# Three products and five adding transfers for each row, in place of four and four

## The chip, the cores and the metric

The kernel runs on one NeuronCore of one Trainium2 chip. The metric is the device time of one execution in microseconds (us), as the median of repeated runs. The engines are named as the profile names them: PE (TensorE, matrix products), PEld (its weight loads), DVE (VectorE), ACT (ScalarE), POOL (GpSimd) and SP (SyncE, here the issuer of plain DMAs).

## The reference, cut to what matters

The model takes 16 rows of 512 tokens with 128 channels through six residual steps. The change touches two of them, both calls of the same mixture of experts, one (k = 0) before a recurrence and one (k = 1) after it:

```python
def _L1_ffn_ref(x, gate_w, w1, w2):              # x: 16 rows x 512 tokens x 128
    scores = jnp.einsum('ntd,ed->nte', x, gate_w)
    probs = jax.nn.softmax(scores, axis=-1)
    g, m = jax.lax.top_k(probs.transpose(0, 2, 1), k)     # 128 of 512 tokens for each of 8 experts
    xin = x[batch_idx, m]
    h = jax.nn.gelu(jnp.einsum('nekd,edf->nekf', xin, w1), approximate=False)
    h = jnp.einsum('nekf,efd->nekd', h, w2)
    out_tok = g[..., None] * h
    return jnp.zeros((n, t, d), dtype=x.dtype).at[batch_idx, m].add(out_tok)
...
x = x + 0.5 * _L1_ffn_ref(_layernorm(x, axis=-1), ...)
```

So for each row and each of its eight experts: 128 chosen tokens are fetched, go through two products with a GELU between, are scaled by their gain, and are added back at the places that they came from.

## The kernel before, in words

The first part of the kernel (to about 970 us) does the attention and the small feed-forward networks of all rows. The change does not touch it. What follows is the expert stage: 2 layers x 16 rows x 8 experts = 256 jobs, and beside them, as side tasks, the recurrence of each pair of rows between the two layers and the routing of the second layer.

A job is one (k, b, e): layer, row, expert. It goes through four stations, one job behind the other, in a loop whose every round has three steps (the three `yield`s at L942, L957 and L988). First, POOL gathers the job's 128 tokens from HBM with an indirect DMA (L859, into xg; issued by `fetch`, ahead of time, about one for each round). PE transposes them two jobs at a time (L883, ps_x), ACT or DVE copies them to xin (L885). PE then makes ps_h (L935), ACT takes the GELU (L937), PE makes ps_y (L950), and ACT scales it by the gain (L953).

The result returns in one of two ways, which `by_product` decides:

- **By product**, for the experts e < EP of each row, and for all eight experts of the very last row. DVE builds a 0/1 matrix from the token numbers (L947), the result is split into three bf16 parts (ACT L953 and L941, DVE L959 and L956), and PE multiplies both in 12 small matmuls that add into the PSUM tile acc (L968). When the row's last product is in, DVE adds acc to x[b] (L972) and SP copies x[b] to a tile in HBM, sums[k, b] (L978).
- **By an adding transfer**, for the other experts. ACT leaves the result in ye, and POOL issues an indirect DMA that adds its 128 rows to sums[k, b] in HBM (L982). After the row's last one, `back` lets 18 steps pass and has SP bring the row back to SBUF (L918, k = 0, after which the row's recurrence may start) or copy it to the output (L923, k = 1).

The order of the jobs is a list that the program makes beforehand (L839 to L846): the products in their order, and behind each product a transfer, beginning EP + 1 products late, so that a row's transfers come after its products. With EP = 4 that is one product and one transfer in turn. Everything is issued in the order of this list: each engine's queue is in order, and the program's own schedule decides the order within it. POOL's queue holds the gathers, the scatters (the adding transfers), and of each normalisation the two steps L293 and L294, which wait for DVE's statistics (L291) and for which DVE's L304 waits. A normalisation of each row precedes its recurrence and another its second routing, four for each pair of rows.

ye has two sets of E - EP slots, used by even and odd rows (L952 and L984). Dependences, between DMAs that touch the same tile in HBM too, become semaphore waits on the queue of the engine that issues.

Of the kernel before, what the change touches and what calls it, by code (L numbers as in the profile page):

```python
# [31 lines left out]
E = 8  # L32
# [3 lines left out]
GB = 8  # L36
IN, OUT = 38, 8
LATE = 28
EP = 4
AHEAD = 4  # L40
EPS = 1e-5
NEG = -1.0e30
# [4 lines left out]
def tile_macaron(  # L47
# [51 lines left out]
    with ExitStack() as ph:  # L99
# [734 lines left out]
        def by_product(k, b, e):  # L834
            return e < EP or (k, b) == (1, B - 1)

# [4 lines left out]
        transfers = [job for job in every if not by_product(*job)]  # L841
        order = []
        for i, job in enumerate(products):
            order.append(job)
            if 0 <= i - EP - 1 < len(transfers):
                order.append(transfers[i - EP - 1])  # L846

        begun, fetched, moved = [0], [0], [0]

# [41 lines left out]
        def experts():  # L891
# [34 lines left out]
            while begun[0] < len(order) or any(line):  # L926
# [16 lines left out]
                if line[1]:  # L943
# [5 lines left out]
                    for f in range(NF):  # L949
                        nc.tensor.matmul(py, lhsT=hs[u][:, f, :], rhs=mw2[e][:, f, :],  # L950
                                         start=(f == 0), stop=(f == NF - 1))
                    yu = yes[u][:, 0, :] if prod[1] else ye[:, b % 2 * (E - EP) + e - EP, 0:D]  # L952
                    nc.scalar.activation(yu, py, AF.Copy, scale=gainT[g][:, n : n + 1])  # L953
# [7 lines left out]
                if prod[3]:  # L961
                    k, b, e, u = line[3]
                    last = E - 1 if (k, b) == (1, B - 1) else EP - 1
                    if e == 0:
# [14 lines left out]
                if line[2] and not prod[2]:  # L979
# [3 lines left out]
                        out=sums[k, b], out_offset=bass.IndirectOffsetOnAxis(ap=tokI[g][:, n : n + 1], axis=0),  # L983
                        in_=ye[:, b % 2 * (E - EP) + e - EP, 0:D], in_offset=None, compute_op=ALU.add,  # L984
                    )
# [244 lines left out]
```

## Time and profile before

| what | value |
|---|---|
| median of 3 runs | 1685.1 us (1683.93 to 1688.63) |
| the profiled execution's own time | 1679.07 us |
| its span, first to last instruction | 1677.3 us |
| granted TensorE clock, mean of the span | 0.979 |
| busy over the span: PE, DVE, ACT, POOL | 94%, 67%, 60%, 61% |
| L968, accumulating matmuls | 1584 (132 jobs x 12), 219 ns each |
| L982, scatters on POOL | 124, 1624 ns each |
| L859, gathers on POOL | 256, 986 ns each |
| first and last start of a scatter | 988.87 and 1667.34 us |

A group's mean duration is that of one instruction. Matmuls overlap in the pipeline, so their mean is longer than the distance between their starts. In a timeline, the brackets hold the time for which the engine stood idle before the instruction and what, by the semaphores, released it; "issue" means that nothing in the profile explains it. Where the named releaser had long been done, it was another, often a DMA.

The page's first two rows of tenths (40 slices of 41.9 us) show PE at nine tenths or more for nearly the whole span, and POOL rising in the expert stage:

```profile
PE   5689999999999999999999799999999999999998
...
POOL 2635557556665556565634757657766668667774
```

### The profile page before, as it was taken

To read this page: it belongs to the slowest core of one execution; us is meant where nothing else is said; L and a number is where in the kernel's file an instruction comes from. 1 tells how busy PE (TensorE), PEld (TensorE's weight loads), DVE (VectorE), ACT (ScalarE), POOL (GpSimd) and SP (SyncE) were. 2 spreads that over 40 slices of the span, in tenths; PEclk is the share of its full clock that TensorE was granted. 3 is DMA by queue.
4 is the path that set the end of the run, shared out by engine and by line. 5 is a ranking of instruction groups with operands and counts; after the bars stand their busy time and mean duration, and the time that the engine had idled before them with its cause. 6 is when DMAs were issued, how large, how long until landed. Compare 5 with 4: busy or idle time off the path is not lost.

```text
span 1677.3 us, 35404 instructions
## 1 busy us (share of the span) xinstructions
PE 1573.0 (94%) x12943; PEld 1093.7 (65%) x12943; DVE 1124.6 (67%) x3606; ACT 1002.3 (60%) x2000; POOL 1023.6 (61%) x1486
## 2 busy tenths in 40 slices
PE   5689999999999999999999799999999999999998
PEld 2234444444444544455444399888998889999998
DVE  6578878888888888888986146843469544672222
ACT  3446677787777877777777565444443434444454
POOL 2635557556665556565634757657766668667774
PEclk9779999999999999999999799999999999999999
DMA  4210111111101110111122114223323233333333
GB/s 123 67 63 26 56 50 40 33 42 57 53 30 40 49 57 23 40 52 56 35 81 62 30 40 78 58 52 76 64 59 64 58 61 73 67 64 75 70 77 58
DMA packets 103093, 94.87 MB, mean 57 GB/s; under 512 B 13197, under 2 KB 91478, under 8 KB 102678
## 3 DMA queue, kind: packets, MB, share of 16 engines
q1 hardware_dynamic: 76060, 67.65, 13.1%
q0 software_dynamic: 26048, 24.93, 9.4%
q8 instruction: 102, 1.67, 0.4%
q14 instruction: 73, 0.60, 0.1%
q10 hardware_dynamic: 810, 0.02, 0.0%
HBM read 59.00 MB, written 37.49 MB: 58 GB/s over the span
## 4 chain that ended last, share of the span: by engine, by line
PE 71%; DVE 19%; ACT 5%; issue 3%; POOL 2%; DMA 1%; DVEq 0%; SPq 0%; POOLq 0%; ACTq 0%
PE ps_h L935 12%; PE ps_y L950 11%; PE ps_av L692 7%; PE ps_st L669 6%; PE ps_sc L611 5%; DVE below L616 5%; PE acc L968 4%; PE ps_kg L365 4%; PE ps_s L338 3%; PE ps_t L318 3%; DVE ln_st L287 2%; ACT pt L672 2%; PE ps_ko L386 2%; PE ps_h L1076 2%; PE ps_h L1075 1%
## 5 line engine op out<-in xcount | busy, mean ns | idle before, releaser
L674 POOL TENSOR_SCALAR_AFFINE_SELECT pt<-pt 128x128 f32<-128x128 f32 (+2 forms) x704 | 252.7, 366 | 331.4 <-ACT pt L672 326.6
L672 ACT ACTIVATE pt<-ps_st 128x512 f32<-128x512 f32 (+1 forms) x704 | 378.8, 563 | 99.8 <-PE ps_st L669 94.0
L616 DVE CUSTOM_DVE_ANT_0 below<-ps_sc,causal 128x512 bf16<-128x512 f32 (+1 forms) x512 | 315.0, 615 | 80.1 <-PE ps_sc L611 64.8
L937 ACT ACTIVATE mo<-ps_h 128x512 f32<-128x512 f32 x256 | 152.8, 597 | 290.4 <-PE ps_h L935 288.5
L859 POOL DMA_INDIRECT xg<-xnd,tokI x256 | 252.3, 986 | 80.9 <-issue 45.0
L669 PE MATMUL ps_st<-qp,kp 99*128 99x512 bf16 (+3 forms) x1024 | 258.5, 305 | 21.7 <-ACT pt L672 20.8
L935 PE MATMUL ps_h<-xin,mw 128*128 128x128 f32 x2048 | 278.3, 279 | 0.0
L950 PE MATMUL ps_y<-mw,mo 128*128 128x128 f32 x2048 | 271.1, 275 | 0.4 <-DVE mo L959 0.4
L611 PE MATMUL ps_sc<-kp,qp 72*128 72x512 bf16 (+3 forms) x1024 | 259.6, 305 | 11.6 <-DVE maxs L616 6.6
L935 PEld LDWEIGHTS ps_h<-xin,mw 128*128 128x128 f32 x2048 | 249.7, 192 | 6.1 <-issue 3.2
L950 PEld LDWEIGHTS ps_y<-mw,mo 128*128 128x128 f32 x2048 | 249.1, 192 | 1.5 <-DVE mo L959 1.3
L982 POOL DMA_INDIRECT sum<-ye,tokI x124 | 201.4, 1624 | 63.4 <-ACT ye L953 22.7
L669 PEld LDWEIGHTS <-kp 99*128 99x128 bf16 x1024 | 95.1, 100 | 181.7 <-issue 164.4
L371 ACT ACTIVATE kan_h<-kan_s,rbias,kw 128x512 f32<-128x512 f32 x256 | 205.7, 812 | 3.8 <-PE ps_kg L365 3.8
L692 PE MATMUL ps_av<-pt,va 128*32 128x512 f32 (+3 forms) x2048 | 165.5, 441 | 0.0
L621 DVE TENSOR_REDUCE maxs<-ps_sc 128x2 f32<-128x512 f32 (+1 forms) x192 | 130.1, 685 | 34.9 <-PE ps_sc L611 34.4
L611 PEld LDWEIGHTS <-qp 72*128 72x128 bf16 x1024 | 96.2, 99 | 79.8 <-issue 57.2
L956 DVE TENSOR_TENSOR mo<-mo 128x128 bf16<-128x128 f32 x132 | 38.2, 290 | 129.4 <-ACT mo L941 129.1
L692 PEld LDWEIGHTS ps_av<-pt,va 128*32 128x32 f32 x2048 | 53.7, 109 | 94.9 <-issue 44.1
L968 PE MATMUL acc<-mo 128*128 128x128 bf16 x1584 | 111.3, 219 | 3.1 <-DVE mo L956 3.0
L968 PEld LDWEIGHTS <-mo 128*128 128x128 bf16 x1584 | 98.6, 98 | 19.9 <-issue 18.6
L294 POOL TENSOR_TENSOR ln_rstd<-ln_rstd,mhalf 128x4 f32<-128x4 f32 x96 | 101.1, 1053 | 8.0
(197 smaller groups left out, 2362.2 us busy)
## 6 DMA issues: line engine op xcount, KB each, us to landing
qp<-qs SPq DMA_DIRECT2D x64, 288.0 KB
xnd<-kan_x SPq DMA_DIRECT2D x32, 256.0 KB
sum<-x SPq DMA_DIRECT2D x31, 256.0 KB
qs<-qpart SPq DMA_DIRECT2D x48, 128.0 KB
kp<-ks SPq DMA_DIRECT2D x48, 96.0 KB
x<-in_L_attn_x_dram SPq DMA_DIRECT2D x16, 256.0 KB
mw<-in_L_ffn_w_dram SPq DMA_DIRECT2D x16, 256.0 KB
xg<-xnd,tokI POOLq DMA_INDIRECT x256
```

The lines of the kernel that those rows point to most:

```text
L371: nc.scalar.activation(h, sk[half], AF.Relu, bias=rbias[:, half, v : v + 1], scale=kw1[:, half, v : v + 1])
L611: nc.tensor.matmul(v[:, u, 0:n], lhsT=qp[r][0 : 9 * HD, g, bass.ts(c, P)], rhs=kp[0 : 9 * HD, r, 0:n], start=alone, stop=(u == len(gs) - 1 ...
L616: nc.vector.tensor_tensor_reduce(below[:, 0:n], v[:, 0, 0:n], causal[:, S - n : S], 1.0, LOWEST, ALU.add, ALU.max, accum_out=maxs[:, c, h ...
L669: nc.tensor.matmul(v[:, u, 0:n], lhsT=kp[ROWS, r, bass.ts(c, P)], rhs=qp[r][ROWS, g, c * P : S], start=True, stop=True)
L672: nc.scalar.activation(o, v[:, :, 0:n], AF.Exp, scale=HD ** -0.5)
L674: nc.gpsimd.affine_select(out=dg, in_=dg, compare_op=ALU.is_ge, fill=0.0, base=0, pattern=[[0, len(gs)], [1, P]], channel_multiplier=-1)
L692: nc.tensor.matmul(po[32 * g : 32 * g + 32, c * P : S], lhsT=va[:, c, r, :], rhs=pt[:, g, OFF[c] : OFF[c] + n], start=(c == 0), stop=(c == ...
L859: nc.gpsimd.indirect_dma_start(out=xgs[i // E % 2][:, i % E, :], out_offset=None, in_=xnd[b], in_offset=bass.IndirectOffsetOnAxis(ap=tokI[ ...
L935: nc.tensor.matmul(pst[:, f, :], lhsT=mw1[e][:, bass.ts(f, P)], rhs=xins[i // E % 2][:, i % E, :], start=True, stop=True)
L950: nc.tensor.matmul(py, lhsT=hs[u][:, f, :], rhs=mw2[e][:, f, :], start=(f == 0), stop=(f == NF - 1))
L968: nc.tensor.matmul(acc[:, c, :], lhsT=sels[u][:, bass.ts(c, P)], rhs=yes[u][:, w, :], start=(e == 0 and c == 0 and w == 0), stop=(e == las ...
L982: nc.gpsimd.indirect_dma_start(out=sums[k, b], out_offset=bass.IndirectOffsetOnAxis(ap=tokI[g][:, n : n + 1], axis=0), in_=ye[:, b % 2 * ( ...
```

## The change

EP becomes 3, so three experts of a row return by product and five by transfer. The order list is filled by a new rule: behind product i come the transfers from number 5 max(i - 4, 0) // 3 up to number 5 max(i - 3, 0) // 3, so that five transfers are queued to three products (one, two and two in turn). The slots of ye follow from EP, two sets of five.

```diff
-EP = 4
+EP = 3
...
         for i, job in enumerate(products):
             order.append(job)
-            if 0 <= i - EP - 1 < len(transfers):
-                order.append(transfers[i - EP - 1])
+            behind = max(i - EP - 1, 0), max(i - EP, 0)
+            order.extend(transfers[slice(*((E - EP) * n // EP for n in behind))])
```

## The prediction

> **What bounds the kernel now.** I first read the windows view over the whole span. Only the expert stage, from about 970 us to the end, executes what the diff touches. Its columns are the window, its length, then busy time and instruction count of PE, PEld, DVE, ACT and POOL, then clock, DMA share and GB/s. Two windows, one of each half:
>
> ```profile
> 1110.00:1150.00 40.00, 40.00 (x356) 36.60 (x354) 17.38 (x69) 15.71 (x38) 26.28 (x25) 1.00 0.34 73
> 1500.00:1650.00 150.00, 150.00 (x1529) 149.62 (x1528) 43.38 (x127) 74.36 (x183) 119.03 (x101) 1.00 0.39 75
> ```
>
> PE is busy without a gap; so the kernel looks PE-bound, and work taken off PE looks like gain. But POOL shows 119 of 150 us with 101 instructions, and the timeline of POOL alone shows what lies between them:
>
> ```profile
> 1603.95 1.67 POOL L982 DMA_INDIRECT sum<-ye,tokI  x1 [0.30 <-ACT mo L941]
> 1605.93 0.98 POOL L859 DMA_INDIRECT xg<-xnd,tokI  x1 [0.31 <-PE ps_y L950]
> 1607.22 0.95 POOL L859 DMA_INDIRECT xg<-xnd,tokI  x1 [0.30 <-issue]
> 1608.47 1.67 POOL L982 DMA_INDIRECT sum<-ye,tokI  x1 [0.30 <-ACT mo L941]
> ```
>
> Every idle time is 0.30 us, whoever is named as its releaser, and half of them are "issue". I read 0.30 as the price of going from one such instruction to the next. Then POOL is full: 119.03 + 101 x 0.30 = 149.3 of 150 us. One pair of jobs (a product and a transfer) costs it a scatter and two gathers, 1.63 + 0.30 + 2 x (0.97 + 0.30) = 4.47 us. From the same windows' PE timeline, one pair costs PE 4.51 us (ps_h at 1601.81, 1606.32, 1610.84). Two engines stand level; the page's POOL share of 61% hides it.
>
> A third reading is the end of that timeline, where no gathers are left:
>
> ```profile
> 1649.11 1.66 POOL L982 DMA_INDIRECT sum<-ye,tokI  x1 [0.30 <-ACT mo L941]
> 1653.28 1.58 POOL L982 DMA_INDIRECT sum<-ye,tokI  x1 [2.51 <-ACT mo L937]
> 1655.16 1.58 POOL L982 DMA_INDIRECT sum<-ye,tokI  x1 [0.30 <-ACT mo L937]
> 1659.20 1.55 POOL L982 DMA_INDIRECT sum<-ye,tokI  x1 [2.46 <-ACT ye L953]
> ```
>
> The first two add into the same row's sum and start 4.17 us apart, though the second one's ye was written by 1649.37 (ACT timeline: 1649.00, 0.37 long) and POOL had nothing else. The third opens another row and follows after 1.88. So a scatter waits until the scatter before it into the same row has landed: the trace's semaphore records end that wait at 1652.55, 3.44 us after the start at 1649.11, and the next scatter starts about 0.7 later. POOL's queue is in order, so gathers behind it wait too.
>
> **The change part by part.** The order of jobs has 101 products and 155 transfers where it had 132 and 124: 31 experts change sides (one for each row but the last of the second layer). In steady state the order is p t | p t t | p t t for each row, instead of p t four times.
>
> *Removed from PE.* For each of the 31, the 12 accumulating matmuls (L968). In PE's timeline they start at 1605.65 and the next ps_h at 1606.32: 0.67 us. 31 x 0.67 = 20.8 us. A row of 8 jobs falls from 4 x 4.51 = 18.06 to 17.4 us.
>
> *Removed from DVE and ACT.* For each: L947, L956, L959 (0.35 + 0.29 + 0.35) on DVE, together 31 us; the L941 cast (0.29) on ACT, 9 us; L953 stays, writing f32 where it wrote bf16, at 0.37 us in both forms. I cost this at nothing: DVE is busy 43 of 150 us and ACT 74 of 150 in the late window, under PE and POOL. Without that cover it could give only what PE waits for them, a few us.
>
> *Added on POOL.* 31 scatters (L982), each 1.63 + 0.30 = 1.93 us: 60 us on an engine without room. A row now asks of POOL 5 x 1.93 + 8 x 1.27 = 19.8 us, over PE's 17.4.
>
> *Added waits.* A transfer next to a transfer has about one gather between the two scatters, since fetch issues one gather for each job (three steps, L865). Their own work lasts 1.93 + 1.27 = 3.20 us, but the wait for the landing holds the second until 3.44 + 0.7 = 4.13. What is queued behind it on POOL are the gathers of later jobs, and in the first layer L293 and L294 of a norm, for which DVE (L304) waits. A transfer with a product between has two gathers and 4.47 us, more than 4.13. A row: 3 x 4.47 + 2 x 4.13 = 21.7 us. Bounds: 19.8 if the wait is free (it is never below, the work is there), 23 if gathers bunch so that two scatters stand bare. I take 21.7, by the rows of both spacings.
>
> Here a rule speaks another way. The Trainium skill, "DMA: Bandwidth & Descriptors", section "Anatomy of one DMA — SWDGE (gpsimd) path", gives about 2.0 us fixed plus bytes / 436e3, nearly all of it completion latency, descriptor generation being small. A scatter of 64 KB would land in 2.15 us and hold POOL for little: then the two adjacent scatters would be 2.85 apart, under their own 3.20, and the row 19.8; and with small generation POOL would not bind at all. The rows say 1.63 us of POOL and 3.44 to landing; I follow them. The same page's "Rules for kernel authors" says an accumulating DMA must wait for an earlier one on the same bytes, which is why the 3.44 us can't be overlapped within a row.
>
> *Copies and SP's queue.* L978 still issues 31 copies into sums, L918 16 and L923 15, so nothing is added. The copy leaves after three products in place of four, and the row's first transfer stands seven places behind the last product where it stood five: the landing of that copy stays covered (7 + 2 - 3 = six rounds of about 2.2 us, since a product is added three rounds after its start and a transfer leaves after two). ye has ten slots in turn where it had eight. L918 and L923 come 18 steps (about six jobs, 13 us) after the last scatter; they cost nothing while POOL's lag stays below that. If it doesn't, L978 of the next row is late behind them.
>
> *The sum, second layer.* Its 60 scatters start from 1389.50 to 1667.34, 277.8 us. After: 15 rows x 21.7 = 325, and two pairs of norms at 2 x (0.23 + 0.08 + 1.04) = 2.7, together 330, less about 1 in the tail without gathers: +51. Gathers end 6.65 us before their transposes, a lead that POOL can lose once before PE stops; it delays the loss and doesn't take it away, as POOL has to issue all scatters before the end. The end itself stays: last scatter to end of span is 10 us as before.
>
> *The sum, first layer.* 988.87 to 1389.50, 400.6 us, where the recurrences give PE more work: a pair of rows takes 49.4 us (scatters at 1120.22 and 1169.62). POOL needed about 41 of these and spent the rest waiting at L293:
>
> ```profile
> 1129.22 0.23 POOL L293 TENSOR_SCALAR ln_rstd<-ln_mv 128x4 f32<-128x4 f32 x1 [7.37 <-DVE ln_mv L291]
> ```
>
> That slack takes the added work. After, PE needs 400.6 - 16 x 0.67 = 389.9, POOL 16 x 21.7 + 14 x 2.7 = 385. Level again, and two engines that wait for each other give away part: between -10.7 and +5, I take -3.
>
> Together +48. The profiled execution reported 1679.1 us (span 1677.3), so it would give 1727; the median of the runs is 6.0 above it, 1685.1, and I add the 48 to that: **1733 us**.
>
> **The rivals.**
>
> *The landing costs nothing* (gathers and norms fill it, or it shortens): 19.8 a row. Second layer 15 x 19.8 + 5 = 302, +24; first layer PE's floor, -10. +14: 1699 us. For it: in a pair with two gathers the wait is hidden today. Against: the 4.17.
>
> *PE stays the bound, faster than before.* The 0.30 us would be slack and not a price: then POOL needs 5 x 1.63 + 8 x 0.97 = 15.9 a row, under 17.4, and all 20.8 us are gained: 1664 us. The point from which it decides is a POOL row of 17.4 us, thus gaps of 0.12 and no landing wait. For it: PE's unbroken 150 us, and releasers named behind many gaps. Against: a gap of exactly 0.30 under any releaser, and in the first layer too, where POOL has slack.
>
> *The lag feeds back.* POOL late in the first layer makes DVE wait at L304 for ln_rstd (today 5.1 us in all), with the products' L947 and L959 behind it, and SP's L918 late. Then the first layer gives +5 to +25 in place of -3: some 1740 to 1765, I put it at 1750.
>
> *Nothing measurable.* The second layer's loss would have to equal the first layer's gain, thus about 18.8 us a row on POOL; no row gives that.
>
> **How the numbers follow.** Likeliest (1733): 0.62. Landing free (1699): 0.16. Feedback (1750): 0.13. PE stays the bound (1664): 0.06. Nothing: 0.03. A measurement of this kernel tells about 0.3% (5 us) from no change. Slower 0.91, same 0.03, faster 0.06. The range holds the likeliest with its bounds (19.8 to 23 a row: -28 to +20), most of the free landing and of the feedback: 1697 to 1762.
>
> **What would show it.** After: L982 x155 near 1.63 us, L968 x1212. In the second layer, PE no longer full (near 80%: 17.4 of 21.7), waiting at ps_x (L883) for the gathers; POOL scatter starts alternating 4.1 and 4.5 us apart; row-to-row about 21.7 between L923s. L293's wait for ln_mv much smaller. Wrong, if PE stays full there, if gaps under 0.30 appear between POOL's DMAs, or if adjacent scatters of one row start 3.2 us apart.

## The result, and the profile after

The changed kernel takes 1742.7 us (median of 4 runs, 1739.96 to 1745.59) where the one before took 1684.6 on the same chip: a ratio of 1.0344 (95% interval 1.032 to 1.0368), 58 us more. The prediction was 1733 us, in a range of 1697 to 1762.

The page of the profiled execution (span 1738.2 us, own time 1739.96), with the rows of tenths and the two groups that the change moves:

```profile
PE   5689999999999999999997997999999999798886
...
POOL 2535646655666555655546567577767677676774
...
L982 POOL DMA_INDIRECT sum<-ye,tokI x155 | 249.9, 1613 | 147.3 <-issue 40.5
...
L859 POOL DMA_INDIRECT xg<-xnd,tokI x256 | 251.5, 982 | 75.6 <-issue 43.5
```

POOL looks no busier than before, 62% of the span. The number to read is the one after the bar: the idle time ahead of L982 went from 63.4 to 147.3 us while a scatter itself kept its 1.6 us. PE has lost its nines at the end. The windows view, with the same two windows as before, says where:

```profile
1110.00:1150.00 40.00, 40.00 (x341) 35.67 (x340) 16.95 (x58) 17.07 (x40) 29.74 (x28) 1.00 0.35 74
1500.00:1650.00 150.00, 124.70 (x1146) 120.83 (x1144) 34.39 (x98) 59.51 (x140) 105.33 (x87) 0.95 0.34 60
```

In the second layer PE falls from 150 to 124.7 of 150 us (83%, where the prediction said near 80%), and POOL's busy time falls too, from 119 to 105. Neither engine is busy all the time, and yet one of them sets the pace. POOL's timeline there:

```profile
1606.25 1.63 POOL L982 DMA_INDIRECT sum<-ye,tokI  x1 [0.30 <-issue]
1608.19 0.98 POOL L859 DMA_INDIRECT xg<-xnd,tokI  x1 [0.30 <-PE ps_y L950]
1609.48 0.95 POOL L859 DMA_INDIRECT xg<-xnd,tokI  x1 [0.30 <-issue]
1610.74 1.62 POOL L982 DMA_INDIRECT sum<-ye,tokI  x1 [0.30 <-ACT mo L937]
1612.67 0.98 POOL L859 DMA_INDIRECT xg<-xnd,tokI  x1 [0.31 <-issue]
1614.84 1.59 POOL L982 DMA_INDIRECT sum<-ye,tokI  x1 [1.19 <-issue]
```

With two gathers between, scatters start 4.49 us apart; with one, 4.10, of which 1.19 is idle time that the profile calls "issue". This wait has a cause although the profile names none: the scatter before it into the same row has not landed. By the trace's semaphore records its last part landed at 1614.08, 0.76 us before the next scatter starts. Over the stage from 1530 us to 25 us before the last scatter, the medians are 4.44 (23 cases) and 4.17 us (15 cases).

PE's waits in the whole stage, after (a wait, its total, its count, its longest):

```profile
PE ps_x L883 <- DMA xg<-xnd,tokI: 38.7, 24, 5.9
PE ps_t L318 <- DVE kan_x L304: 14.1, 9, 8.6
```

and before:

```profile
PE acc L968 <- DVE mo L956: 3.0, 8, 0.9
PE ps_x L883 <- DMA xg<-xnd,tokI: 1.2, 1, 1.2
```

PE now waits for gathers that POOL issues late, and in the first layer for a normalisation behind L304.

### The profile page after: what moved, and what is told of

It is laid out like the page before. It is cut to its first block, busy times and chain, and to the rows that moved or that the text cites. A ratio compares the mean times of both kernels' runs of the same rounds, so it can differ in the third digit from the quotient of the medians.

```text
span 1738.2 us, 34532 instructions
## 1 busy us (share of the span) xinstructions
PE 1577.3 (91%) x12571; PEld 1086.9 (63%) x12571; DVE 1101.3 (63%) x3513; ACT 999.9 (58%) x1969; POOL 1070.5 (62%) x1517
## 5 line engine op out<-in xcount | busy, mean ns | idle before, releaser
L982 POOL DMA_INDIRECT sum<-ye,tokI x155 | 249.9, 1613 | 147.3 <-issue 40.5
L935 PE MATMUL ps_h<-xin,mw 128*128 128x128 f32 x2048 | 282.7, 282 | 0.0
L669 PE MATMUL ps_st<-qp,kp 99*128 99x512 bf16 (+3 forms) x1024 | 258.9, 305 | 21.6 <-ACT pt L672 20.7
L950 PE MATMUL ps_y<-mw,mo 128*128 128x128 f32 x2048 | 277.6, 280 | 0.4 <-DVE mo L959 0.4
L935 PEld LDWEIGHTS ps_h<-xin,mw 128*128 128x128 f32 x2048 | 254.5, 195 | 19.9 <-issue 12.5
L950 PEld LDWEIGHTS ps_y<-mw,mo 128*128 128x128 f32 x2048 | 257.1, 197 | 0.6 <-DVE mo L959 0.5
L959 DVE SCALAR_TENSOR_TENSOR mo<-ps_y,gainT,mo 128x128 f32<-128x128 f32 x101 | 34.5, 341 | 144.8 <-ACT mo L953 144.6
L294 POOL TENSOR_TENSOR ln_rstd<-ln_rstd,mhalf 128x4 f32<-128x4 f32 x96 | 100.7, 1049 | 8.0
L318 PE MATMUL ps_t<-ident,kan_x 128*128 128x128 f32 x384 | 68.3, 297 | 40.4 <-DVE kan_x L308 24.0
L883 PE MATMUL ps_x<-ident,xg 128*128 128x128 f32 x256 | 55.6, 285 | 38.9 <-DMA xg<-xnd,tokI 38.7
```

What stands on the lines that cost most here:

```text
L669: nc.tensor.matmul(v[:, u, 0:n], lhsT=kp[ROWS, r, bass.ts(c, P)], rhs=qp[r][ROWS, g, c * P : S], start=True, stop=True)
L935: nc.tensor.matmul(pst[:, f, :], lhsT=mw1[e][:, bass.ts(f, P)], rhs=xins[i // E % 2][:, i % E, :], start=True, stop=True)
L982: nc.gpsimd.indirect_dma_start(out=sums[k, b], out_offset=bass.IndirectOffsetOnAxis(ap=tokI[g][:, n : n + 1], axis=0), in_=ye[:, b % 2 * ( ...
```

## The experiments

Theory A is the prediction's: POOL's row of scatters, gathers and landing waits sets the pace, and PE's gain is real but hidden. In e1 and e2, A's figures were set from the trace of the changed kernel, and what the prediction had summed stands there as rival B. The rivals are named in the expectations. "Row" below is the distance between the starts of two rows' L972 on DVE, or of two scatters of the same number on POOL where that is said. Each ratio is against the kernel before on the same chip. The first four shared a chip (before 1680.7 us there), the next four another (1682.4), the last four a third (1712.0).

**Second layer alone (e1).** EP is 4 in the first layer and 3 in the second, with the order filled by the same rule:

```diff
-            return e < EP or (k, b) == (1, B - 1)
+            return e < EPS_OF[k] or (k, b) == (1, B - 1)      # EPS_OF = (4, 3)
...
+        def due(k, b, e):
+            own = EPS_OF[k]
+            return first[k, b] + own - (-own * (e - own + 1) // (E - own))
```

> Four and four in the first layer, three and five in the second. Theory A (POOL's row of 21.7 us sets the second layer, and the first layer loses by its own): first to last scatter of the second layer goes from 292.4 us to about 335, the first layer stays at 386 within 3, the time is about 1728 us (+43). Rival B (what the prediction summed: +51 in the second layer, -3 in the first): 1736 us. Rival C (the first layer's lag carries over and makes the second layer's loss): under 1705 us.

Measured: 1727.95 us, ratio 1.0294 (1.0275 to 1.0313). The first layer, by its scatters, took 384.9 us, the second 342.0 from first to last scatter. The second layer loses by itself; rival C falls. The 47 us over the kernel before lie between A's 43 and B's 51 and don't tell these two apart; e2 does.

**First layer alone (e2).** The same with EPS_OF = (3, 4).

> Three and five in the first layer, four and four in the second. Theory A: the first layer alone loses, because POOL's lag makes DVE wait for ln_rstd (L304): about +18 us, 1703 us, with L304's wait for L294 near the 33 us of the full change. Rival B (the prediction's sum): -3 us, 1682 us, L304 waiting little more than its 5 us of before.

Measured: 1693.75 us, ratio 1.0088 (1.0072 to 1.0105), so +13 us: nearer to A than to the prediction's sum of -3, and under both A's 18 and its L304 wait (21.7 us where 33 was expected). The first layer loses too.

**Two rows in turn (e3).** Neighbouring transfers go to different sums:

```diff
+        transfers.sort(key=lambda job: (job[0], job[1] // 2, job[2], job[1]))
...
-            behind = max(i - EP - 1, 0), max(i - EP, 0)
+            behind = max(i - 2 * EP - 1, 0), max(i - 2 * EP, 0)
```

> The changed kernel with the transfers of two rows taken in turn, so that neighbours in the order add into different sums and don't wait for each other; each row's transfers start three products later. Theory A (an adjacent scatter waits for the landing of the one before it, 4.13 us against 3.20 of work): steady rows of the second layer fall from 21.7 to about 19.8 us, the second layer from 336 to about 308, the time to about 1715 us. Rival D (POOL's own work or the gathers' landing sets the row, not the scatters' landing): rows stay at 21.7 and the time at 1743 us.

Measured: 1732.15 us, ratio 1.0307 (1.0283 to 1.033): under the changed kernel's 1.0344 (1.032 to 1.0368), but the intervals touch, so a gain is not certain, and it is far from the 28 us. The second layer did as A said: 310.3 us between its first and last scatter, rows of 19.5, 19.9 and 19.7 us late in it. But the first layer, from its first scatter to the second layer's first, grew to 413.5 us. Part of this is the border itself, which moves when transfers start three products later. And PE stopped 8.1 us for a gather that came at 1331 us; that the rows finished later and so the routing came late is the likely reason, not tested by itself. Two effects in one run; e8 parts them.

**Two scatters left out (e4).**

```diff
-                if line[2] and not prod[2]:
+                if line[2] and not prod[2] and line[2][2] not in (EP + 1, EP + 3):
```

> The changed kernel without the scatters of experts 4 and 6, so the results of these two experts are left out of the sum; their products stay. POOL then needs 3 x 1.93 + 8 x 1.27 = 16 us a row. Theory A: PE's gain of 0.67 us an expert is real and only POOL hides it: PE is full again, steady rows of the second layer take 17.4 us, the time is about 1664 us (-21). Rival E (the products' removal gives PE nothing, as other waits take its place): about 1685 us, rows of 18.06.

Measured: 1666.66 us, ratio 0.9913 (0.9896 to 0.993). Its window late in the second layer, same columns:

```profile
1500.00:1600.00 100.00, 100.00 (x993) 99.80 (x993) 25.70 (x71) 51.09 (x123) 76.13 (x67) 1.00 0.35 77
```

PE is full again and steady rows take 17.3 us. With POOL relieved the removed products give what they were priced at (14 of the 18 to 21 us in the time; 18.1 to 17.3 in the row). Rival E falls.

**The kernel before with one more gather a row (e5).**

```diff
                     if e == E - 1:
+                        nc.gpsimd.indirect_dma_start(
+                            out=ye[:, 8 + b % 2, 0:D], out_offset=None, in_=xnd[b],
+                            in_offset=bass.IndirectOffsetOnAxis(ap=tokI[g][:, n : n + 1], axis=0),
+                        )
                         sides.append(back(k, b))
```

> The kernel before, with one more gather for each row behind its last scatter (its 128 rows land in a place that nothing reads). PE's work is unchanged; POOL gets 31 x 1.27 us. Theory A (PE and POOL stand level before the change, 18.06 and 17.9 us a row): steady rows of the second layer go to about 19.2 us, the time rises by some 12 to 18 us. Rival F (PE alone bounds the kernel before): rows stay at 18.06 and the time at 1681 to 1685 us.

Measured: 1699.51 us, ratio 1.0105 (1.0066 to 1.0144), +17 us; later rows of the second layer 18.7 to 20.6, most of them 19.0 to 19.4. PE's row of the waits from 1530 us on:

```profile
PE ps_x L883 <- DMA xg<-xnd,tokI: 4.7, 13, 0.9
```

An instruction of 1 us on an engine that the page shows at 61% cost more than half of its own length each time. Rival F falls: PE was full before, and POOL stood level with it.

**The first normalisation's L304 later (e6, and e10 once more).** The profile after shows one stop of PE in the first layer above all. On DVE and on PE:

```profile
1061.94 1.12 DVE L304 TENSOR_SCALAR kan_x<-x,ln_mv,ln_rstd 128x128 f32<-128x128 f32 x4 [9.52 <-POOL ln_rstd L294]
```

```profile
1062.34 0.99 PE L318 MATMUL ps_t<-ident,kan_x 128*128 128x128 f32 x3 [8.63 <-DVE kan_x L304]
```

POOL reached L293 at 1060.5 us, 11 us after its statistics were ready; DVE stood at L304 with the products' steps queued behind it, and PE ran dry. The experiment moves L304 of the first pair back in the order:

```diff
-            yield from rest(1)
+            yield from rest(wait)          # 14 for the first pair, else 1
```

> The changed kernel, with the kan_x step (L304) of the first pair's first normalisation put 13 steps later in the order, about 10 us. POOL's work and its order are the same. Theory A (the first layer's loss is in the main one stop: POOL reaches L293 11 us late, DVE waits 9.5 us at L304 with the products' steps behind it, PE stops 8.6 us and then has half its clock for 10.2 us): the stop and the slow stretch go, 10 to 14 us less, about 1730 us. Rival G (POOL's total sets the first layer, and the stop only moves): 1743 us.

Measured: 1732.88 us, ratio 1.0288 (1.0254 to 1.0321), which touches the change's 1.032 to 1.0368; its profiled execution had a span of 1737.7. Unclear, so both were run side by side.

> The changed kernel as it is, on one chip with the next three, to compare the later L304 with it directly: 1742 us within 5.

> The changed kernel with the first pair's L304 put 13 steps later, once more, as its first median was 10 us lower while its profiled execution was not (1737.7 against 1738.2 us). Theory A (the stop is the loss): 10 us under the changed kernel of the same call. Rival G (the stop only moves, as the profile showed it at 1099 us with 4.2 us): within 4 us of it.

Measured: the changed kernel 1742.59 us, the later L304 1740.13; ratios 1.0189 (1.0166 to 1.0212) and 1.0167 (1.0145 to 1.0188). In e10 PE's waits for L304 in the first layer fell from 11.6 to 7.9 us, the longest 4.3 and now at 1099 us. Rival G's forecast holds: the stop moves and the time stays within 4 us. That POOL's work sets the first layer is the reading that fits; the run shows only that this stop doesn't.

**Odd rows of the first layer only (e7).** The same rule as in e1, with `3 if k == 0 and b >= 4 and b % 2 else 4`.

> Three and five only for the odd rows from 5 on of the first layer, where POOL had 8 us of slack in each pair of rows; all else four and four. Theory A: 6 scatters more cost POOL 12 to 18 us that its slack there takes up, PE gains 6 x 0.67 = 4.0 us: 1677 to 1681 us beside 1681 to 1685 of before. Rival (any added scatter costs, through the lag at the norms): 0 to +5 us over before.

Measured: 1685.34 us, ratio 1.0009 (0.9994 to 1.0023). No gain that can be told, against the 4 us expected: the slack of 8 us in a pair of rows doesn't pay even for every other row. It was the attempt at a version faster than both; none of these runs, of those that compute all, is one.

**Two rows in turn, second layer only (e8).** e1 with its transfers ordered as in e3 in the second layer, but for the last pair of rows.

> Four and four in the first layer; three and five in the second, with the transfers of two rows in turn there, so that neighbours add into different sums. To be compared with the same without the turns (1728 us). Theory A (the landing wait costs 0.93 us at each of two adjacent scatters in a row, about 28 us over 15 rows): about 1700 to 1706 us, steady rows 19.8 in place of 21.7. Rival D (the landing of the scatters isn't what holds POOL): 1728 us.

Measured: 1704.89 us, ratio 1.0138 (1.0102 to 1.0174), 23 us under e1's 1727.95 (which ran on another chip, with before at 1680.7 beside 1682.4). POOL's timeline in it:

```profile
1614.96 1.62 POOL L995 DMA_INDIRECT sum<-ye,tokI  x1 [0.30 <-ACT xin L898]
1616.89 0.99 POOL L872 DMA_INDIRECT xg<-xnd,tokI  x1 [0.30 <-issue]
1618.18 1.59 POOL L995 DMA_INDIRECT sum<-ye,tokI  x1 [0.30 <-issue]
```

L995 is the scatter and L872 the gather here. With one gather between and another row's sum as the target, two scatters start 3.22 us apart; over 14 cases the median is 3.21 and the maximum 3.22. It was 4.17 into the same sum. Same instructions, same engine, another target: the landing wait is shown, at 0.96 us a time by these medians. Rival D falls.

**The normalisations off POOL (e11, e12).** The kernel before, and e2's kernel, with the two POOL steps on DVE in the expert stage:

```diff
-            nc.gpsimd.tensor_scalar_add(rstd, mv[:, :, 1], EPS)
-            nc.gpsimd.tensor_tensor(rstd, rstd, mhalf, ALU.pow)
+            if hurry[0]:
+                nc.vector.tensor_scalar_add(rstd, mv[:, :, 1], EPS)
+                nc.vector.reciprocal(rstd, rstd)
...
```

> The kernel before, with the two POOL steps of each normalisation in the expert stage (L293, L294) done on DVE as an add and a reciprocal; this takes 1 / (var + eps) where 1 / sqrt(var + eps) is wanted, which changes values and no amount of work behind it. POOL loses 64 x 1.35 us of work and its waits for L291. As PE is full in the first layer, both theories expect little: 1675 to 1683 us. It is the control of the next.

> Three and five in the first layer, four and four in the second, with the normalisations' steps on DVE as in the control (1 / (var + eps) for the inverse root). POOL's row of 21.7 us is then under PE's 23.5 in the first layer, and nothing of DVE waits for POOL. Theory A (the first layer loses because POOL's lag reaches DVE and PE through L293 and L294, and through their work on POOL): PE's 0.67 us an expert comes out, 5 to 11 us under the control. Rival G (the first layer loses by the scatters themselves, gathers coming late): 5 to 13 us over the control.

Measured: 1703.28 us for the control, ratio 0.9945 (0.9926 to 0.9963), and 1692.66 for three and five in the first layer, ratio 0.9896 (0.9869 to 0.9923): 10.6 us under its control, where the same change with the normalisations on POOL cost 13. The size is A's, but it doesn't decide. The 13 was measured on another chip; on this one the kernel before and the control lay 20 to 30 us higher than expected and the changed kernel did not (see the last section), and the first layer's change with its normalisations on POOL was not run here. Nor does it tell apart POOL's work of L293 and L294 from the waits through them, since both went.

## Why the prediction was right in its sign, and where it was off

Point by point, by its own steps.

*PE's 0.67 us an expert.* Right, and hidden as said: e4.

*The 0.30 us as a price, POOL level with PE.* Right: e5, and the after profile has the same gap throughout.

*The second layer's row.* Predicted 21.7 us; the first scatters of rows late in the second layer start 21.6 to 22.6 us apart, with one at 23.7. The prediction's two spacings, 4.47 and 4.13, measured 4.44 and 4.17. The rule that the Trainium skill gives in "DMA: Bandwidth & Descriptors", section "Anatomy of one DMA — SWDGE (gpsimd) path" (by its fit, an estimate of 2.15 us for such a transfer, so no wait) would have made the row 19.8. The scatters of this trace landed 3.39 us after their start (median), and rows took 19.5 to 19.9 us only when e3 aimed neighbours at different sums (in e8 18.4 to 21.3, 19.9 on average). The rows of the trace were right to be followed.

*Where the layers meet.* The prediction took 1389.50 us as the second layer's first scatter. That was the second one; the first (the 65th) starts at 1374.94. How the 60.9 us between the two profiled spans are shared out depends on this border. From the first scatters, the first layer went from 386.1 to 404.2 us (+18.2) and the second, to its last scatter, from 292.4 to 335.7 (+43.3). From the second ones, the border that the prediction used, it is +10.8 and +50.7. (The rest is +1.1 ahead of the first scatter and -1.7 behind the last.) Neither border is clean: in e2 the first scatters would give the unchanged second layer -8. e1 and e2 need no border: the second layer alone costs 47 us and the first alone 13. So the second layer's part of the prediction held: +51 for +50.7 by its own border and for +47 alone; with the first scatter as border, its own sum would be 15 x 21.7 + 3 x 2.7 - 1 = 333 us, for 335.7 measured.

*The first layer's -3.* This step failed: +11 to +18 by the borders, +13 in e2. The prediction counted on POOL's slack there, and the slack was used up. POOL's waits at L293 from 985 us to the end of the first layer, before and after:

```profile
POOL ln_rstd L293 <- DVE ln_mv L291: 59.9, 14, 9.2
POOL ln_rstd L293 <- DVE ln_mv L291: 7.8, 5, 2.9
```

With the first scatter as border and so 13 pairs of norms, POOL's sum is 16 x 21.7 + 13 x 2.7 = 382 for 404.2 measured. Where the missing 22 us stand, the POOL timeline tells: what exceeds 0.30 us in the idle times ahead of L982 adds up to 50.4 us in the first layer (7.4 before), where two landing waits of 0.93 in each row make 30. The semaphore records say what these waits are. In 32 of them, 41.7 us together, the scatter starts 0.72 to 0.79 us after the last part of the scatter before it has landed: 12 us more than was summed. The other 8.6 us are four waits that ended 1.7 to 2.1 us after that landing; their cause is open. So the largest part of the mis-sized sum, 12 of the 22 us, is the landing, taken at 3.44 us everywhere. Its median is 3.39, but it is longer at times:

```profile
1295.99 1.53 SPq L741 DMA_DIRECT2D xnd<-kan_x  x2
1297.39 1.62 POOL L982 DMA_INDIRECT sum<-ye,tokI  x1 [0.30 <-issue]
1298.27 0.36 SPq L978 DMA_DIRECT2D sum<-x  x1
1299.32 1.00 POOL L859 DMA_INDIRECT xg<-xnd,tokI  x1 [0.31 <-PE ps_y L950]
1303.69 1.59 POOL L982 DMA_INDIRECT sum<-ye,tokI  x1 [3.38 <-ACT ye L953]
```

The named releaser is wrong again: this scatter's ye was written by 1293.3. By the semaphore records, fifteen of the sixteen parts of the scatter before it had landed by 1301.45; the last one came at 1302.94, 5.55 us after the start. Three copies of SP, 256 KB each, left in between or just ahead, and they are the first suspect. But the DMA view from 1297 to 1303 us has another:

```profile
q8 instruction: 1, 0.02, 1.9%
```

This is one transfer of 16 KB on a queue that the profile calls "instruction"; it took 1.8 us, from 1299.35 on. In the profile after, 145 scatters have all sixteen parts on record. In 17 of them the last part came more than 0.5 us behind the fifteenth, and each of the 17 had such an instruction transfer under way between the end of its work on POOL and its landing; of the other 128, 25 had. Over all fourteen traces it is 109 of 109 late ones and 256 of 1181 others. A copy of SP, from 6 us before the scatter on, was there in 82 of the 109 and in 743 of the 1181. So the instruction transfers fit the late parts better than the copies do. That they cause them is argued from this, not shown: no run took either away.

*The feedback rival.* The prediction gave it 0.13, +5 to +25 in the first layer and 1750 us. The first layer's +13 lies there, and 1743 is nearer to 1750 than to 1733. But its mechanism is only half right. DVE did wait for POOL at L304 (33.0 us in all, from 5.1), and PE behind it; yet where the worst of these stops was taken away (e10), the time stayed within 4 us. As far as e10 shows, the stops are how PE comes to know of POOL's lag, not what makes the time.

*Level engines give away a part.* Right in kind: in the first layer PE's idle time from 985 us to the second layer's first L972 rose from 3.2 to 16.4 us.

The +48 was 10 us short of the +58 of the medians and 13 short of the 60.9 of the spans. By the prediction's own border the second layer was met (+51 for +50.7) and the whole miss is the first layer, 14 too few. By e1 and e2 it is 4 too many and 16 too few, which in part cancelled; so much of the total's nearness is luck.

## What to carry to other kernels

Count an engine's fixed gap between instructions as work before calling it idle: late in the second layer POOL, at 61% over the span, was full, and so work taken from the full PE and put on POOL lost. Where DMAs add into the same place, their landing is a serial chain, and the engine that issues them stands in it with all that is queued behind; aiming neighbours at different places won back 23 us here (e8). And take the price of a wait from many of its cases, not from one clean one: the median landing was as priced, and about one in eight was late.

## What was not expected of the hardware

The granted clock of TensorE fell after its stops. In the profile after, the clock record shows half speed for 10.2 us from 1057.1 on, inside and behind PE's stop of 8.63 us, for 3.4 or 6.8 us in six places of the second layer, and once more from 1729.6 us to the end. In the kernel before there was none in the expert stage until its last 1.4 us. Two windows of the changed kernel, the clock in the third column from the end:

```profile
1040.00:1060.00 20.00, 13.71 (x140) 13.49 (x138) 11.30 (x41) 7.12 (x16) 14.38 (x13) 0.93 0.35 59
1056.00:1068.00 12.00, 5.50 (x26) 4.62 (x27) 5.37 (x17) 1.81 (x4) 9.76 (x11) 0.57 0.35 72
```

The first seven of these slow stretches each follow a stop of PE of 2.2 to 8.6 us; four other stops, of 2.5 to 3.2 us, were followed by none. What the slow stretches cost beside the stops themselves was not measured.

The kernel before is not equally fast on all chips: medians of 1684.6, 1680.7, 1682.4 and, on the last chip, 1712.0 us (12 runs, 1706.55 to 1714.1), while the changed kernel took 1742.7 and 1742.6 on the first and the last. The ratio is 1.0189 on that chip. No trace of the kernel before was taken there, so the cause stays open. The control e11, on the same chip, had scatters with two gathers between 4.89 us apart on average (29 cases, longest 6.36), where the kernel before had 4.53 (24 cases, longest 4.96). Longer landings don't explain this: the median landing of the second layer's scatters was 3.26 us there and 3.39 in the kernel before. POOL waited for ye instead: of the fourteen scatters from 1500 to 1690 us that it stood idle for by more than 0.5 us, eleven started 0.28 us after ACT had written their ye. So POOL did not hold that control; what made PE and ACT late is not known.
